# Graph attention on one core: index work in even steps only, edge rows turned between the last node operations

## The chip, the core and the metric

The kernel runs on one core of a Trainium2 chip. Five engines work side by side, each through its own list of instructions in order: TensorE (PE in the profile; PEld are its weight loads), VectorE (DVE), ScalarE (ACT), GpSimd (POOL) and SyncE (SP), which here only issues transfers. The metric is the device time of one execution in microseconds.

## What is computed

6250 nodes with 256 features and 200,000 edges, sorted by destination. The input goes through a layer norm and a Relu to h; then come two layers of graph attention over the edges, with four heads of 64 and with one of 256, and residuals:

```python
def _gat(x, src, dst, ea, Wg, a_s, a_d, Wge, a_e, b, n, h, f):
    hx = (x @ Wg).reshape(n, h, f)
    he = (ea @ Wge).reshape(-1, h, f)
    al = leaky_relu(einsum(hx, a_s)[src] + einsum(hx, a_d)[dst] + einsum(he, a_e), 0.2)
    m = segment_max(al, dst)
    al = exp(al - m[dst])
    al = al / segment_sum(al, dst)[dst]
    out = segment_sum(hx[src] * al[:, :, None], dst)
    return out.reshape(n, h * f) + b
...
te = relu(edge_attr @ We0 + be0) * exp(x @ Wo0 + bo0)[src][:, None]
s2, d2, ea2 = _add_self_loops(src, dst, te, n)
x = relu(_gat(x, s2, d2, ea2, Wg0, ...) + x)
...
x = _gat(x, s2, d2, ea2, Wg1, ...) + x
return x + orig
```

A node's own edge (the self loop) carries the mean of its edges' features.

## The kernel before

A prologue computes the table T of node rows for layer 0 (the 256 transformed features and a few attention terms) and keeps it in HBM. Then each layer goes over the edges in 66 steps: 64 steps of 24 chunks with 128 edges each, and two shorter ones. Every chunk column holds one edge per partition. The method edges (L792) writes out the work of a step k (st) together with preparations for step k + 1 (nx) and what is left of step k - 1 (pv) and k - 2 (late); since the schedule is manual, every engine's list is in the order of that code.

What a step does, in the order of the code, with the engine:

- gather (L1065): 24 indirect transfers, issued on POOL at L1084, bring the source rows of a step's edges from T into one of three buffers G. Since POOL's list runs ahead, it fills the buffer for step k + 2 as soon as the sums of step k - 1 have released it.
- logits (L1367, VectorE): the attention logits al of 24 x 128 edges from G, from rt and from ade, then two scans along the edges (L1390 and L1392) for running maxima per destination.
- ends (L1396, TensorE): turns the last values of each partition into lf.
- spread and parts (VectorE): for a pair of steps at once, in the step before an even one, spread (L1198) builds the one-hots lb (L1210) and Q (L1211) by which destination terms reach the edges; parts (L1315) cuts the destination terms into three bf16 parts (L1325 to L1328). So they stand in odd steps only. TensorE's first product into zad (L1333) waits for them.
- rphase1, rphase2 and adst (TensorE and ScalarE): edge features of step k + 1 through the edge weights, into zad.
- links and maxima (L1401 and L1418, VectorE and TensorE): scans over partitions (L1409, L1411) that read lf, then the maximum per destination; exp on ScalarE.
- scale (L1474, VectorE, L1481) multiplies G by the weights; carried adds what the step before left open; onehots (L1312) builds S, the one-hots of the destinations.
- sums (L1485, TensorE, L1493): 24 products of S and G, each in two passes (48 rows in the trace), summed in PSUM as u; evict copies u on ScalarE.
- the node stage for the step before: finish, which is nodes0 in layer 0 (L1547; merge, then VectorE with one Relu on ScalarE); rows1 to rows3 turn the finished rows and multiply them into the table of layer 1. node_x (L1655) writes x + h into the same row tile t1rows, which goes to HBM.
- edge_rows (L1350, VectorE): turns zad of step k + 1 to rt (L1361) and sums three parts to ade (L1364).

Besides, VectorE prepares index data for the whole of both layers in layer 0: index_group (L738) turns destinations and next destinations of four steps (a group) into the tables loc, flpen, pen and isl, in 14 small operations, most of them 128 x 96. They lie in a generator; index_on (L871), called at the end of a step, issues seven of them. The group is loaded (index_load) when the next group is two steps off or less (left <= 2), which is in every fourth step, k = 0, 4, 8. So seven operations stand at the end of that step, between the node stage and edge_rows, and the rest at the end of the next, odd, step. The logits that follow on VectorE belong to steps k + 1 and k + 2.

Of the kernel before, what the change touches and what calls it, by code (L numbers as in the profile page):

```python
# [81 lines left out]
class Kernel:  # L82
# [425 lines left out]
    def first_edges(self, st, f):  # L508

        if f == 11:  # L510
            st["y"] = self.rphase1(st)
            next(st["y"])
        if f == 12:
            self.spread(st)
            self.parts(st)
        if f == 14:
            self.blocks(st)
            drain(st["y"])
            self.load_ea(1)
        if f == 16:  # L520
            self.rphase2(st)
            self.adst(st)
        if f == 18:
            self.edge_rows(st)
# [213 lines left out]
    def index_group(self, g, pool, di):  # L738
# [8 lines left out]
        t = pool.tile([P, 4 * C], F32, name="gt", bufs=2)  # L747

        def v3(x):
            return x.rearrange("p (s c) -> p s c", c=c)  # L750
# [4 lines left out]
        d3, t3 = v3(dst), v3(t[:, :w])  # L755
        base = self.base_f[:, ss[0]:ss[0] + n].unsqueeze(2).to_broadcast([P, n, c])
        V.tensor_sub(t3, d3, base)
        yield
        V.tensor_scalar(self.loc[:, o:o + w], t[:, :w], 255.0, None, op0=OP.min)
        yield  # L760
        ends = self.before[:, ss[0]:ss[0] + n].unsqueeze(2), v3(dnx)[:, :, c - 1:]
        for pen, e in zip((self.fpen, self.lpen), ends):
            t = pool.tile([P, 4 * C], F32, name="gt", bufs=2)
            e3 = e.to_broadcast([P, n, c])
            V.tensor_sub(v3(t[:, :w]), *((d3, e3) if pen is self.fpen else (e3, d3)))
            yield
            V.tensor_scalar(pen[:, o:o + w], t[:, :w], 1.0, -BIG, op0=OP.min, op1=OP.mult)
            yield
        t = pool.tile([P, 4 * C], F32, name="gt", bufs=2)
        t3 = v3(t[:, :w])  # L770
        V.memset(t3[:, :, 0:1], 1.0)
        V.tensor_sub(t3[:, :, 1:], d3[:, :, 1:], d3[:, :, :c - 1])
        yield
        V.tensor_scalar(self.pen[:, o:o + w], t[:, :w], 1.0, -BIG, op0=OP.min, op1=OP.mult)
        yield
        t = pool.tile([P, 4 * C], F32, name="gt", bufs=2)
        V.tensor_sub(t[:, :w], dnx, dst)
        yield
        V.tensor_scalar(self.isl[:, o:o + w], t[:, :w], 1.0, None, op0=OP.min)
        yield  # L780
        V.tensor_scalar(t[:, :w], t[:, :w], 0.0, None, op0=OP.is_lt)
        yield
        V.tensor_reduce(self.bad[:, 1 + g:2 + g], t[:, :w], axis=AX.X, op=OP.add)
# [8 lines left out]
    def edges(self, ctx):  # L792
# [6 lines left out]
        for k, st in enumerate(steps):  # L799
# [54 lines left out]
            if pv:  # L854
                drain(self.finish(pv))
# [4 lines left out]
            self.index_on(left)  # L860
# [5 lines left out]
            self.edge_rows(nx)  # L866
# [19 lines left out]
    def ending(self, a, b, c, pv, late, after):  # L886
# [43 lines left out]
        self.edge_rows(b)  # L930
# [27 lines left out]
        self.edge_rows(c)  # L958
# [68 lines left out]
        if after:  # L1027
# [22 lines left out]
            self.edge_rows(after)  # L1050
# [299 lines left out]
    def edge_rows(self, st):  # L1350
# [6 lines left out]
        if c % 2:  # L1357
            for w, o in self.halves(st):
                V.transpose(rv[:, w], z[:, o])
        else:  # L1360
            V.transpose(rv[:, :32 * c].rearrange("p (b n) -> p b n", b=2),  # L1361
                        z.rearrange("p (b n) -> p b n", b=2)[:, :, :16 * c])
        st["ade"] = ade = self.wp.tile([P, C, 4], F32, name="ade")
        V.tensor_reduce(ade[:, :c, :H], rt[:, :c, 4:4 + 3 * H].rearrange("p c (h t) -> p c h t", t=3),  # L1364
                        axis=AX.X, op=OP.add)

# [180 lines left out]
    def nodes0(self, st, wp, e=None):  # L1547
# [23 lines left out]
        e.tensor_add(b, a, b)  # L1571
# [4 lines left out]
        yield  # L1576
        st["trow"] = self.trow1[st["s"] % 3]
        if "lag" not in st:
            yield from self.node_x(st, e)
# [18 lines left out]
    def nodes1(self, st, wp, e=None):  # L1598
# [6 lines left out]
        yield  # L1605
# [171 lines left out]
def drain(g):  # L1777
    for _ in g:
        pass
# [85 lines left out]
```

## Time and profile before

| what | value |
|---|---|
| median of 3 runs | 4735.77 us (4732.58 to 4746.24) |
| profiled execution | 4693.76 us, of which the span of the trace 4692.0 |
| mean granted TensorE clock | 0.744 |
| HBM traffic | 591.77 MB, 126 GB/s over the span |
| VectorE instructions | 6211, 2864.4 us busy |
| scale (L1481) | 149 operations, 854.1 us |
| sums (L1493) | 6212 rows, 1719.5 us |
| gathers (L1084) | 3066 issues of 953 ns |

A row of the timeline reads: start in us, duration in us, engine, line, operation, out<-in, shapes, count, and in brackets how long the engine was idle before it and what ended that by the trace; "issue" is a wait for nothing that the trace shows. A row of the view by stretches has, behind the bounds and the length, busy us (and number) of PE, PEld, DVE, ACT and POOL, the granted TensorE clock, the DMA engines' share and GB/s. A row of the view of waits has the total, the number of waits and the longest. Ends of TensorE's rows are modelled, their starts are measured. Line numbers are those of the kernel before.

### The profile page before, as it was taken

Reading aid. Unit: us, or ns where it says so; the run is one execution under the profiler, and the core shown is the slowest. Engines: PE = TensorE matmul, PEld = TensorE weight load, DVE = VectorE, ACT = ScalarE, POOL = GpSimd, SP = SyncE. Lnnn points to the kernel's source line nnn. Section 1 sums busy time; section 2 is a strip of 40 time slices with the busy share of each in tenths; the row PEclk is TensorE's granted clock in tenths of the full one; section 3 lists DMA queues with packets and bytes.
Section 4 is the critical chain, followed back from the end, with each engine's and each line's share of the span. In section 5 each row is a group of like instructions: output and inputs, shape, how many; then the busy total and the mean of one; then the engine's idle time right before and its main releaser. Section 6 shows DMA issues by size and latency. Waiting matters only on the chain.

```text
span 4692.0 us, 35121 instructions
## 1 busy us (share of the span) xinstructions
PE 2924.1 (62%) x10096; PEld 1849.2 (39%) x10096; DVE 2864.4 (61%) x6211; ACT 531.9 (11%) x1189; POOL 2996.0 (64%) x3216
## 2 busy tenths in 40 slices
PE   7666666666666666666666665665556566565666
PEld 5433343343334334344344343333334334333333
DVE  6666676666666666676675554545555455554546
ACT  4211111111111111111110000000000000000000
POOL 5466666666666666666646666666666666666664
PEclk8877777777777777777788676667777766776667
DMA  7344444444444444444444444444444444444442
GB/s 223 89 133 130 127 131 136 123 136 137 124 134 135 125 134 138 125 133 134 122 123 123 118 120 121 124 120 118 126 115 123 122 124 119 118 125 114 122 127 74
DMA packets 248234, 591.77 MB, mean 126 GB/s; under 512 B 65849, under 2 KB 105125, under 8 KB 247783
## 3 DMA queue, kind: packets, MB, share of 16 engines
q0 software_dynamic: 150048, 422.51, 34.5%
q1 hardware_dynamic: 97009, 164.82, 10.9%
q10 hardware_dynamic: 976, 2.12, 0.2%
q8 instruction: 81, 1.33, 0.1%
q14 instruction: 120, 0.98, 0.1%
HBM read 544.23 MB, written 45.36 MB: 126 GB/s over the span
## 4 chain that ended last, share of the span: by engine, by line
DVE 41%; PE 22%; issue 17%; another core or an unknown queue 15%; POOL 2%; ACT 1%; DMA 1%; DVEq 0%; ACTq 0%
DVE G L1481 14%; PE u L1493 14%; DVE S L1312 5%; PE y L1186 3%; POOL G L1084 2%; DVE rt L1361 2%; DVE lb L1210 1%; DVE m L1431 1%; PE ps L570 1%; PE zad L1195 1%; DVE cl L1409 1%; DVE cl L1411 1%; PE fin L570 1%; DVE t1rows L1659 1%
## 5 line engine op out<-in xcount | busy, mean ns | idle before, releaser
L1084 POOL DMA_INDIRECT G<-T,src x3066 | 2920.4, 953 | 1589.9 <-issue 886.1
L1493 PE MATMUL u<-G,S 128*128 128x270 f32 (+1 forms) x6212 | 1719.5, 436 | 700.3 <-issue 501.6
L1493 PEld LDWEIGHTS u<-G,S 128*128 128x128 f32 x6212 | 1324.7, 216 | 1042.7 <-issue 532.5
L1481 DVE TENSOR_TENSOR G<-G,kps 128x6144 f32<-128x6144 f32 (+6 forms) x149 | 854.1, 5739 | 0.0
L1186 PE MATMUL y<-ea,webd 64*128 64x256 f32 (+2 forms) x1056 | 452.1, 799 | 402.8 <-issue 395.1
L1409 DVE TENSOR_TENSOR_SCAN cl<-fl,cl,lf 4x129 f32<-4x129 f32 (+1 forms) x130 | 61.1, 470 | 901.1 <-remote 547.7
L1312 DVE TENSOR_TENSOR S<-kps,loc 128x3072 f32<-128x3072 f32 (+1 forms) x135 | 438.0, 3245 | 4.6
L1195 PE MATMUL zad<-R,wea 128*64 128x384 f32 (+1 forms) x1056 | 294.3, 697 | 154.8 <-ACT R L1187 97.2
L1186 PEld LDWEIGHTS y<-ea,webd 64*128 64x128 f32 x1056 | 159.7, 281 | 531.5 <-issue 519.6
L1499 ACT ACTIVATE U<-u 128x270 f32<-128x270 f32 (+1 forms) x130 | 51.2, 394 | 2037.2 <-remote 1168.4
L1187 ACT ACTIVATE R<-y,webd 128x1024 f32<-128x1024 f32 (+3 forms) x264 | 235.4, 892 | 368.2 <-PE y L1186 169.4
L1195 PEld LDWEIGHTS zad<-R,wea 128*64 128x64 f32 x1056 | 85.0, 181 | 411.9 <-ACT R L1187 205.9
L1361 DVE STREAM_TRANSPOSE rt<-zad 128x768 f32<-128x768 f32 (+1 forms) x130 | 125.8, 968 | 0.8 <-PE zad L1347 0.8
L570 PE MATMUL fin<-wg,h1T 128*128 128x260 f32 x264 | 124.2, 619 | 3.1 <-ACT h1T L1586 3.1
L1333 PE MATMUL zad<-a,Q 128*128 128x12 bf16 (+1 forms) x132 | 24.0, 182 | 156.0 <-issue 81.4
L1399 PE MATMUL lf<-ident,fb 128*36 128x128 f32 (+1 forms) x132 | 44.1, 334 | 112.4 <-DVE fb L1392 51.1
L1210 DVE TENSOR_TENSOR lb<-lb,kps 128x1536 bf16<-128x1536 bf16 (+1 forms) x68 | 112.9, 1660 | 0.0
L1584 PE MATMUL fin<-ident,fb 128*128 128x128 f32 x132 | 43.2, 385 | 82.3 <-issue 81.2
L1524 ACT ACTIVATE mw<-mw,mg 128x2 f32<-128x2 f32 x66 | 19.7, 298 | 607.7 <-DVE mw L1520 390.8
L1416 PE MATMUL lf<-ident,cl 36*128 36x36 f32 (+1 forms) x132 | 38.7, 293 | 76.6 <-DVE cl L1411 76.2
L1347 PE MATMUL zad<-lb,aq 128*128 128x384 bf16 (+2 forms) x264 | 86.0, 419 | 0.0
L1416 PEld LDWEIGHTS lf<-ident,cl 36*128 36x128 f32 (+1 forms) x132 | 22.9, 173 | 158.2 <-DVE cl L1411 155.4
(264 smaller groups left out, 2273.4 us busy)
## 6 DMA issues: line engine op xcount, KB each, us to landing
ea<-in_ea_dram SPq DMA_DIRECT2D x64, 768.0 KB
G<-T,src POOLq DMA_INDIRECT x3066
lb<-locrow SPq DMA_DIRECT2D x64, 384.0 KB
nd<-t1rows SPq DMA_DIRECT2D x66, 225.8 KB
tw<-nd SPq DMA_DIRECT2D x66, 225.8 KB
tw<-T SPq DMA_DIRECT2D x66, 117.2 KB
T<-t1rows SPq DMA_DIRECT2D x66, 113.8 KB
tw<-in_x_dram SPq DMA_DIRECT2D x66, 112.0 KB
```

The lines of the kernel that those rows point to most:

```text
L570: self.product = self.nc.tensor.matmul(ps[:, :L.MW], hT[:, k, :], self.wg[L.l][:, k, :], start=(k == 0), stop=(k == 1))
L1084: g = nc.gpsimd.indirect_dma_start(out=G[:, c, 0:L.TW], out_offset=None, in_=st.get("from", self.T[L.l])[0:self.N, :], in_offset=bass.Indi ...
L1186: nc.tensor.matmul(y[:, i, :n], self.webd[l][r, :], ea[r, w], start=True, stop=True)
L1187: nc.scalar.activation(R[:, :, w], y[:, :, :n], AF.Relu, bias=self.be[l])
L1195: nc.tensor.matmul(st["zad"][i * PH:(i + 1) * PH, o], self.wea[l][0], R[:, i, w], start=True, stop=False)
L1210: V.tensor_tensor(lb[:, :, :n], lb[:, :, :n], self.k_part.unsqueeze(2).to_broadcast([P, i, n]), op=OP.is_equal)
L1312: nc.vector.tensor_tensor(st["S"][:, c0:c1, :], self.k_iota.unsqueeze(1).to_broadcast(w), self.loc[:, o + c0:o + c1].unsqueeze(2).to_broad ...
L1347: self.nc.tensor.matmul(st["zad"][:, o], st["aq"].rearrange("p k j -> p (k j)"), st["lb"][:, w], start=False, stop=True)
L1361: V.transpose(rv[:, :32 * c].rearrange("p (b n) -> p b n", b=2), z.rearrange("p (b n) -> p b n", b=2)[:, :, :16 * c])
L1409: V.tensor_tensor_scan(cl[:H, :], fl[:H, :], lf[:H, 0:P + 1], init, op0=OP.add, op1=OP.max)
L1481: nc.vector.tensor_tensor(v, v, pw[:, c0:c1, :].unsqueeze(3) .to_broadcast([P, c1 - c0, H, L.F]), op=OP.mult)
L1493: p = nc.tensor.matmul(st["u"][:, :L.W], S[:, i, :], G[:, i, 0:L.W], start=(j == 0), stop=(j == c - 1))
```

## The change

1. Index work is issued elsewhere. index_on is called twice in a step: once behind logits and ends, where it acts only in even steps, and once where it stood, where it acts only in the first two steps and when a group must be finished. The load is issued a step earlier (left <= 3).
2. The 14 operations are ordered anew, so that hardly any stands right behind one that it needs: three subtractions first, then three that use them, and so on. The third temporary is the memory of the loaded indices.
3. edge_rows is a generator with a stop behind the transposes and one behind the reduction. finish says where a gap may be filled (yield True), and edges puts the two pieces into the gaps of the node stage; in the other places edge_rows is drained at once.
4. In nodes0 the Relu reads the sum in a (fa) and writes b (fb). The row for layer 1 is made by one operation that clamps a itself and adds x + h, in place of an addition that reads the Relu's result.

```diff
-            if self.rest is None and left <= 2:
+            self.fresh = self.rest is None and left <= 3
+            if self.fresh:
                 gi = self.index_load(self.ahead, self.xp)
...
                 drain(self.logits(st))
                 self.ends(st)
+                self.index_on(k, left, False)
             self.spread(nx)
...
-            if pv:
-                drain(self.finish(pv))
+            rows = self.edge_rows(nx)
+            for gap in self.finish(pv) if pv else ():
+                if gap:
+                    next(rows, None)
+            drain(rows)
             self.evict(st)
...
-            self.index_on(left)
+            self.index_on(k, left, True)
...
-            self.edge_rows(nx)
...
-    def index_on(self, left):
-        if self.rest is not None:
-            for _ in range(7):
-                next(self.rest, None)
-            if left <= 0:
-                drain(self.rest)
-                self.ahead, self.rest = self.ahead + 1, None
+    def index_on(self, k, left, late):
+        if self.rest is None or (left > 0 and k > 1 if late else k % 2 or k < 2 or self.fresh):
+            return
+        for _ in range(7):
+            next(self.rest, None)
+        if left <= 0:
+            drain(self.rest)
+            self.ahead, self.rest = self.ahead + 1, None
...
         e.tensor_add(a, a, hw)
         yield
-        e.tensor_add(b, a, b)
-        if e is V:
-            self.nc.scalar.activation(b, b, AF.Relu)
-        else:
-            e.tensor_scalar(b, b, 0.0, None, op0=OP.max)
-        yield
         st["trow"] = self.trow1[st["s"] % 3]
+        nrow = st["trow"][:, self.L[1].TW:self.L[1].TW + D]
         if "lag" not in st:
-            yield from self.node_x(st, e)
+            e.tensor_add(nrow, xw, hw)
+        yield True
+        e.tensor_add(a, a, b)
+        self.nc.scalar.activation(b, a, AF.Relu)
+        yield True
+        if "lag" not in st:
+            e.scalar_tensor_tensor(nrow, a, 0.0, nrow, op0=OP.max, op1=OP.add)
```

Two places of VectorE's list show it. The first is the end of the node stage in the first step of a group; before, from the last sum of the node stage (fb) over the index operations (gf, gt, loc, flpen) to the edge rows (rt, ade):

```order
L1571 TENSOR_TENSOR fb<-fa,fb 128x256
L1659 TENSOR_TENSOR t1rows<-tw_203,hw 128x256
L1661 TENSOR_TENSOR t1rows<-t1rows,fb 128x256
L752 CAST gf<-gi 128x192
L757 TENSOR_TENSOR gt<-gf,base 128x96
L759 TENSOR_SCALAR loc<-gt 128x96
L765 TENSOR_TENSOR gt<-gf,before 128x96
L767 TENSOR_SCALAR flpen<-gt 128x96
L765 TENSOR_TENSOR gt<-gf 128x96
L767 TENSOR_SCALAR flpen<-gt 128x96
L1361 STREAM_TRANSPOSE rt<-zad 128x768
L1364 TENSOR_REDUCE ade<-rt 128x96
```

The same place after the change; the numbers of the lines are those of the changed kernel, in which logits begin at L1377:

```order
L1571 TENSOR_TENSOR fa<-fa,hw 128x256
L1576 TENSOR_TENSOR t1rows<-tw_203,hw 128x256
L1361 STREAM_TRANSPOSE rt<-zad 128x768
L1578 TENSOR_TENSOR fa<-fa,fb 128x256
L1365 TENSOR_REDUCE ade<-rt 128x96
L1582 SCALAR_TENSOR_TENSOR t1rows<-fa,t1rows 128x256
L1377 TENSOR_TENSOR G<-rt,G 128x24x4
L1379 TENSOR_TENSOR al<-G 128x24x4
```

The seven index operations are gone from here, and transposes and reduction each have a node operation behind them. The second place is that between the logits of an even step and its links (cl); before, for a step that is the first of a group:

```order
L1377 TENSOR_TENSOR al<-G 128x24x4
L1379 TENSOR_TENSOR al<-al,ade 128x24x4
L1381 SCALAR_TENSOR_TENSOR al<-al 128x96
L1390 SCALAR_TENSOR_TENSOR fb_195<-pen_183,al 128x96
L1392 SCALAR_TENSOR_TENSOR fb_195<-pen_183,al 128x96
L1409 SCALAR_TENSOR_TENSOR cl_189<-fl,cl_190,lf 4x129
```

And after the change, again in a step that is the first of a group:

```order
L1394 SCALAR_TENSOR_TENSOR fb_195<-pen_183,al 128x96
L751 CAST gf<-gi 128x192
L760 TENSOR_TENSOR gt_6389<-gf,base 128x96
L760 TENSOR_TENSOR gt_6390<-gf,before 128x96
L760 TENSOR_TENSOR gi<-gf 128x96
L762 TENSOR_SCALAR loc<-gt_6389 128x96
L765 TENSOR_SCALAR flpen<-gt_6390 128x96
L765 TENSOR_SCALAR flpen<-gi 128x96
L1411 SCALAR_TENSOR_TENSOR cl_189<-fl,cl_190,lf 4x129
```

Seven operations now stand in front of links; the other seven stand at the same place two steps later. The lists of TensorE and POOL keep their order. On SP the two loads of the indices stand a step earlier.

More of the change, by code (lines that the diff above doesn't have):

```diff
@@ L754, in index_group @@
         dst, dnx = df[:, 0, :w], df[:, 1, :w]
-        d3, t3 = v3(dst), v3(t[:, :w])
+        d3 = v3(dst)
         base = self.base_f[:, ss[0]:ss[0] + n].unsqueeze(2).to_broadcast([P, n, c])
-        V.tensor_sub(t3, d3, base)
-        yield
-        V.tensor_scalar(self.loc[:, o:o + w], t[:, :w], 255.0, None, op0=OP.min)
-        yield
[L761 to L765, printed above, removed]
-            yield
-            V.tensor_scalar(pen[:, o:o + w], t[:, :w], 1.0, -BIG, op0=OP.min, op1=OP.mult)
-            yield
@@ L769, in index_group @@
[L769 to L772, printed above, removed]
+        first = self.before[:, ss[0]:ss[0] + n].unsqueeze(2).to_broadcast([P, n, c])
+        end = v3(dnx)[:, :, c - 1:].to_broadcast([P, n, c])
+        t = [pool.tile([P, 4 * C], F32, name=f"gt{i}", bufs=1)[:, :w] for i in range(2)] + [di[:, 0, :w].bitcast(F32)]
+        for x, y, z in zip(t, (d3, d3, end), (base, first, d3)):
+            V.tensor_sub(v3(x), y, z)
+            yield
@@ L1049, in ending @@
                 next(fill, None)
-            self.edge_rows(after)
+            drain(self.edge_rows(after))
             drain(fill)
```

30 lines of the change are left out of this document (17 added, 13 removed).

## The prediction

> **What bounds the kernel now.** The page comes first: the busy share of each engine and the chain that ended last.
>
> ```profile
> PE 2924.1 (62%) x10096; PEld 1849.2 (39%) x10096; DVE 2864.4 (61%) x6211; ACT 531.9 (11%) x1189; POOL 2996.0 (64%) x3216
> DVE 41%; PE 22%; issue 17%; another core or an unknown queue 15%; POOL 2%; ACT 1%; DMA 1%; DVEq 0%; ACTq 0%
> ```
>
> No engine is full, and a third of the chain is waiting. So the question is how long a step takes and what ends it. The view by stretches, one stretch of layer 0 and one of layer 1:
>
> ```profile
> 437.41:2339.74 1902.33, 1198.07 (x4052) 755.67 (x4051) 1269.88 (x2788) 230.47 (x541) 1232.80 (x1297) 0.76 0.47 131
> 2588.04:4577.04 1989.00, 1204.61 (x4006) 743.41 (x4006) 1069.63 (x2031) 152.56 (x291) 1327.54 (x1392) 0.70 0.45 121
> ```
>
> POOL issues 24 gathers a step, so these are 1297 / 24 = 54 steps of layer 0 at 35.23 us and 1392 / 24 = 58 steps of layer 1 at 34.29 us. VectorE is busy 23.5 us of a step in layer 0 and 18.4 us in layer 1: 5 us more work costs only 0.94 us. The excess is not spread evenly, as POOL's first gather of five successive steps shows in the timeline (the last column is POOL's wait before it):
>
> ```profile
> 1001.36 0.94 POOL L1084 DMA_INDIRECT G<-T,src  x1 [4.73 <-PE fin L1584]
> 1035.69 0.94 POOL L1084 DMA_INDIRECT G<-T,src  x1 [4.65 <-PE fin L1584]
> 1073.18 0.94 POOL L1084 DMA_INDIRECT G<-T,src  x1 [7.85 <-PE fin L1584]
> 1107.50 0.94 POOL L1084 DMA_INDIRECT G<-T,src  x1 [4.35 <-PE fin L1584]
> 1142.30 0.94 POOL L1084 DMA_INDIRECT G<-T,src  x1 [5.05 <-PE u L1493]
> ```
>
> The steps last 34.33, 37.49, 34.32 and 34.80 us. POOL fills the third gather buffer and must wait until the sums on TensorE (u<-G,S) have released it, so its restart marks the end of a step's sums. I call that moment the restart. What happens before it, in an ordinary step, on TensorE:
>
> ```profile
> 1084.78 13.44 PE L1493 MATMUL u<-G,S 128*128 128x270 f32 x46 [4.56 <-DVE crow L1469]
> 1100.62 0.61 PE L1493 MATMUL u<-G,S 128*128 128x270 f32 x1 [2.40 <-issue]
> 1103.43 0.61 PE L1493 MATMUL u<-G,S 128*128 128x270 f32 x1 [2.20 <-issue]
> ```
>
> The sums start 11.6 us after the restart at 1073.18. 46 of the 48 run at 0.29 us each, until 25 us after the restart; then one takes 2.8 us, though it waits for nothing that is shown. This slow stretch ends shortly before the next restart, and layer 1 has it too, there with the next step's first products in it:
>
> ```profile
> 3506.94 0.58 PE L1186 MATMUL y<-ea,webd 64*128 64x256 f32 x1 [2.64 <-issue]
> 3513.00 0.95 POOL L1084 DMA_INDIRECT G<-T,src  x1 [4.54 <-remote]
> ```
>
> VectorE is slow in it as well, wherever an operation waits for its own predecessor. Sums that start in time end inside the stretch and cost nothing more; sums that start late have a remainder behind it. That is the long step:
>
> ```profile
> 1050.94 8.70 PE L1493 MATMUL u<-G,S 128*128 128x270 f32 x37 [1.51 <-DVE crow L1469]
> 1068.67 4.23 PE L1493 MATMUL u<-G,S 128*128 128x270 f32 x8 [1.49 <-issue]
> ```
>
> Its sums start 15.25 us after the restart, eight are left at 1068.67, and the next restart comes 3.2 us late. Why they start late is told by VectorE around that restart:
>
> ```profile
> 1025.31 0.26 DVE L757 TENSOR_TENSOR gt<-gf,base 128x96 f32<-128x96 f32 x1 [2.83 <-issue]
> 1026.71 0.21 DVE L759 TENSOR_SCALAR loc<-gt 128x96 bf16<-128x96 f32 x1 [1.14 <-issue]
> 1028.81 0.27 DVE L767 TENSOR_SCALAR flpen<-gt 128x96 bf16<-128x96 f32 x1 [1.73 <-remote]
> 1031.62 0.21 DVE L767 TENSOR_SCALAR flpen<-gt 128x96 bf16<-128x96 f32 x1 [2.38 <-issue]
> 1031.75 0.98 DVE L1361 STREAM_TRANSPOSE rt<-zad 128x768 f32<-128x768 f32 x1
> 1036.41 0.33 DVE L1392 TENSOR_TENSOR_SCAN fb<-pen,al 128x96 f32<-128x96 bf16 x1
> 1036.66 1.73 DVE L1210 TENSOR_TENSOR lb<-lb,kps 128x1536 bf16<-128x1536 bf16 x1
> 1039.34 0.47 DVE L1409 TENSOR_TENSOR_SCAN cl<-fl,cl,lf 4x129 f32<-4x129 f32 x1
> ```
>
> Seven index operations of a quarter of a microsecond stand in the slow stretch, four of them behind one that they need, and those wait 8.08 us together. Edge rows and logits come after them, the logits end 0.7 us behind the restart, and then the spread of an odd step stands before links: links' first scan (cl) starts 3.65 us after the restart. Two and three steps on it starts 0.15 and 0.40 us after the restart:
>
> ```profile
> 1107.65 0.47 DVE L1409 TENSOR_TENSOR_SCAN cl<-fl,cl,lf 4x129 f32<-4x129 f32 x1
> 1137.28 0.34 DVE L1392 TENSOR_TENSOR_SCAN fb<-pen,al 128x96 f32<-128x96 bf16 x1
> 1142.70 0.47 DVE L1409 TENSOR_TENSOR_SCAN cl<-fl,cl,lf 4x129 f32<-4x129 f32 x1 [5.09 <-PE zad L1333]
> ```
>
> The first of these rows is the odd step without index work before it, with the same spread; in the even step at 1142 VectorE stands idle for 5.09 us between logits and links.
>
> **The change part by part.** *Index work moved.* Of each group of four steps, the second (odd) one no longer has seven index operations ahead of its edge rows. Its logits and its spread can then end as in the odd step at 1107, so that links start at the restart and the sums 11.6 us after it, as at 1084.78. POOL's waits at the first and the last of the 14 long steps of this kind between 437 and 2340 us are:
>
> ```profile
> 509.51 0.94 POOL L1084 DMA_INDIRECT G<-T,src  x1 [7.98 <-PE u L1493]
> 2339.74 0.94 POOL L1084 DMA_INDIRECT G<-T,src  x1 [6.46 <-PE u L1493]
> ```
>
> An ordinary wait is that of layer 1, in the view of who waited for whom in the same stretch as above:
>
> ```profile
> POOL G L1084 <- remote: 149.7, 34, 4.6
> POOL G L1084 <- PE y L1186: 95.2, 22, 4.8
> ```
>
> 244.9 us over 56 waits are 4.37 us. The three long steps quoted stand 3.61, 3.48 and 2.09 us above it, 3.06 on average: 14 x 3.06 = 43 us less. The bounds: all of the excess of layer 0 is 54 x 0.94 = 51 us in this stretch, so the long steps can't give more than that; taking only the cheapest of the three, 14 x 2.09 = 29 us.
>
> *Index work added behind the even steps' logits.* There, VectorE is free for 5.09 us, TensorE being busy with sums, transposes and lf. Seven operations at one per 1.4 us (the spacing of the rows at 1025.31 and 1026.71) would need 9.8 us if all lay in the slow stretch; 5.09 / 1.4 = 3.6, so about four fit before it ends, and three are left for 3 x 0.27 = 0.8 us beside TensorE's own last pieces. What waits behind them on VectorE is the links scan, and behind that TensorE's transposes, the scale and the sums. Cost: 0 to 0.8 us in each of the 27 even steps of the 54, 0 to 22 us; I take 0.1 us, 3 us in all, since the next part makes the cover longer. Without that cover the seven cost 7 x 0.27 = 1.9 us.
>
> *Edge rows between the last node operations.* Before, in the order of VectorE:
>
> ```profile
> 1126.26 0.44 DVE L1571 TENSOR_TENSOR fb<-fa,fb 128x256 f32<-128x256 f32 x1
> 1127.97 0.43 DVE L1661 TENSOR_TENSOR t1rows<-t1rows,fb 128x256 f32<-128x256 f32 x1 [0.94 <-DVE t1rows L1659]
> 1128.31 0.98 DVE L1361 STREAM_TRANSPOSE rt<-zad 128x768 f32<-128x768 f32 x1
> 1130.70 0.45 DVE L1364 TENSOR_REDUCE ade<-rt 128x96 f32<-128x288 f32 x1 [1.41 <-DVE rt L1361]
> 1133.51 0.32 DVE L1377 TENSOR_TENSOR al<-G 128x96 f32<-128x96 f32 x1 [2.18 <-issue]
> ```
>
> The count stays the same. The wait for the Relu on ScalarE (0.94 us in front of L1661; the view names the operation before it) goes, since the last node operation clamps by itself, and the reduction no longer stands behind its transposes (1.41 us): logits start up to 2.4 us earlier. On the path this counts only where logits and spread are late without index work. One such step:
>
> ```profile
> 824.79 0.94 POOL L1084 DMA_INDIRECT G<-T,src  x1 [4.40 <-PE fin L1584]
> 826.78 0.47 DVE L1409 TENSOR_TENSOR_SCAN cl<-fl,cl,lf 4x129 f32<-4x129 f32 x1
> 860.49 0.95 POOL L1084 DMA_INDIRECT G<-T,src  x1 [5.78 <-PE u L1493]
> ```
>
> Links start 1.99 us after the restart, and POOL's next wait is 1.41 us above the ordinary one. The excess that the long steps leave is 51 - 43 = 8 us; I take 6 us of it. The Trainium skill speaks against this part (VectorE: DVE Perf Modes, "The DRAIN you can't avoid" and "Rules for kernel authors"): a chain with a semaphore after each operation is said to take as long as one without, so only the number of operations counts, not their distance. By that rule this term would be 0 and the sum 6 us smaller; the waits of 1.41 and 2.18 us in the slow stretch of this trace differ from it.
>
> *The rest.* Relu reads a and runs later on ScalarE, in front of the eviction, which waits for the sums anyway: 0. The index loads are issued a step earlier, and SP's queue has no wait behind them that others wait for: 0. TensorE's and POOL's orders don't change. In layer 1, VectorE has 16 us free a step: 0.
>
> The sum: 43 - 3 + 6 = 46 us. The profiled execution took 4693.76 us (span 4692.0) and would take 4648. The median of the runs shown is 4735.77, 42 us more, and no view shows where these lie; I take the same 46 us off it: 4690 us, 1.0% faster.
>
> **The rivals.** *Slower: the index work comes too late in the even steps.* If it were issued only after the slow stretch ends, together with what logits still owe, links would start as late in 27 even steps as now in the long ones, +3.06 us each: 27 x 3.06 - 46 = 37 us more, 4773 us. For it speaks that the logits of the other even step of a group have no such gap in front of links; they end 0.14 us behind the restart at 1073.18:
>
> ```profile
> 1072.99 0.33 DVE L1392 TENSOR_TENSOR_SCAN fb<-pen,al 128x96 f32<-128x96 bf16 x1
> ```
>
> Against it: they are late because index work stood before their edge rows in the long step, and just that goes. It decides from 46 / 27 = 1.7 us of delay per even step.
>
> *No change: POOL sets the pace.* POOL is the busiest engine at 64%; 34.33 us of an ordinary step less its wait of 4.65 are 29.7 us of gathers, which the change leaves alone, and if they set the step the time stays at 4736 us. The Trainium skill says as much (Perfetto Trace Analysis, "Identifying the Most-Contended Engine": the engine with the highest occupancy is the one to optimise first). Against it: POOL's own wait grows from 4.65 to 7.85 us just where links is late, so there POOL is held by TensorE. A delay of 1.7 us in the even steps gives this time too.
>
> *The spread alone makes odd steps long.* Then moving index work would give only the 6 us of the third part and lose 3: 4733 us. The odd step at 1107 with its spread and 34.80 us speaks against it.
>
> **The numbers.** About 0.3% (14 us) is what a measurement can tell. Forecast, a gain of more than 14 us: 0.87; POOL or the spread: 0.09; slower: 0.04. The range: the cheapest long steps less the dearest even steps leave 29 - 22 = 7 us, 4729; I stop at the border of no change, 4722, which leaves 1.3 in 10 above; the lower end is all excess of layer 0 (57 steps, with three alike before the stretch: 54 us), and 14 us more, as far as the runs of this kernel lie apart: 4735.77 - 54 - 14 = 4668.
>
> **What would show it.** Right: POOL restarts in layer 0 every 34.2 to 34.8 us, with no step of 37; links' first scan within 0.7 us of the restart in every step; logits ended 3 us or more before it; index operations between them and links, in even steps alone; layer 1 unchanged at 34.29. Wrong: even steps of 36 us with VectorE busy at the restart, or odd steps still long with the spread as what links follows.

## The result, and the profile after

The changed kernel takes 4694.35 us (median of 4 runs, 4690.43 to 4703.82), the kernel before beside it 4734.88 us (4732.58 to 4746.24): ratio 0.9913, 95% interval 0.99 to 0.9925, 40.5 us less. The forecast was 4690 us. The profiled execution of the changed kernel took 4691.18 us (span 4689.3), in line with its other runs. That of the kernel before had taken 4693.76 us, 41 us under its median. So the two traces are only 2.7 us apart, and where the time went must be read from the steps, not from the spans.

The page of the changed kernel, busy time and chain:

```profile
PE 2936.1 (63%) x10096; PEld 1851.6 (39%) x10096; DVE 2834.2 (60%) x6211; ACT 534.1 (11%) x1189; POOL 3000.1 (64%) x3216
DVE 31%; PE 24%; issue 19%; another core or an unknown queue 14%; POOL 10%; ACT 1%; DMA 1%; SPq 0%; DVEq 0%; ACTq 0%; POOLq 0%
```

VectorE's share of the chain fell from 41% to 31%, and POOL's rose from 2% to 10%. The view by stretches, between the restarts that answer to those of before:

```profile
439.45:2323.49 1884.04, 1188.67 (x4050) 748.92 (x4048) 1257.19 (x2778) 230.30 (x541) 1235.44 (x1296) 0.76 0.48 133
2574.56:4573.76 1999.20, 1215.24 (x4006) 747.55 (x4006) 1054.42 (x2031) 154.95 (x291) 1328.86 (x1392) 0.71 0.44 120
```

54 steps of layer 0 take 34.89 us each (35.23 before): 18.3 us less in this trace. 58 steps of layer 1 take 34.47 us (34.29 before), 10.2 us more. There too the edge rows now stand between the last two node operations, but VectorE stands idle in front of links for 15.86 us (before, at 3512.80), so its order should not count. The median even step of layer 0 rose by as much, from 34.32 to 34.49 us. So 0.18 us a step is taken below for a difference between the two executions; no run shows that it is one. POOL's restarts in the timeline of the changed kernel, at the place that was quoted of before and at one that did worse:

```profile
683.37 0.94 POOL L1084 DMA_INDIRECT G<-T,src  x1 [4.82 <-PE u L1495]
719.89 0.94 POOL L1084 DMA_INDIRECT G<-T,src  x1 [6.83 <-PE u L1495]
...
1035.33 0.94 POOL L1084 DMA_INDIRECT G<-T,src  x1 [5.72 <-PE u L1495]
1069.99 0.94 POOL L1084 DMA_INDIRECT G<-T,src  x1 [4.97 <-PE fin L1587]
1104.42 0.94 POOL L1084 DMA_INDIRECT G<-T,src  x1 [4.52 <-PE fin L1587]
1139.68 0.94 POOL L1084 DMA_INDIRECT G<-T,src  x1 [5.20 <-PE u L1495]
```

The step at 1035, a long one of 37.49 us before, lasts 34.66 us; the odd step at 1104 without index work, 34.80 us before, lasts 35.26 us, and the one of that kind at 683 lasts 36.52. Taken together by their place in a group of four, from all 54 steps of each trace:

| place in a group of four | steps | before, mean us | after, mean us | all of them, us |
|---|---|---|---|---|
| even, ahead of the long step | 14 | 34.35 | 34.67 | +4.6 |
| odd, the long step before | 14 | 37.20 | 34.79 | -33.8 |
| even, behind the long step | 13 | 34.33 | 34.65 | +4.2 |
| odd, with the spread but no index work before | 13 | 34.95 | 35.47 | +6.8 |

Behind the means lie two kinds of steps: 39 of the 54 last 34.37 to 34.95 us after the change, 15 last 35.17 to 36.57. Seven of the 15, all of the last kind in the table, have sums that start late, 11.9 us or more after the restart. In the other eight, five of them even, the sums start on time, 11.2 to 11.5 us after the restart; but only 40 to 44 of the 48 run at the full rate, and two or three are left at the end. Such sums, in the even step of 35.67 us that starts at 1835.42:

```profile
1846.59 9.38 PE L1495 MATMUL u<-G,S 128*128 128x270 f32 x40 [1.23 <-issue]
...
1869.31 1.51 PE L1495 MATMUL u<-G,S 128*128 128x270 f32 x3 [1.49 <-issue]
```

VectorE behind the logits of an even step and at the end of the next (odd) one, in the timeline of the changed kernel:

```profile
1065.98 0.33 DVE L1394 TENSOR_TENSOR_SCAN fb<-pen,al 128x96 f32<-128x96 bf16 x1
1066.24 0.24 DVE L768 TENSOR_TENSOR gt<-gf 128x92 f32<-128x92 f32 x1
1069.43 0.21 DVE L772 TENSOR_SCALAR pen<-gt 128x96 bf16<-128x96 f32 x1 [2.78 <-remote]
1069.80 0.25 DVE L778 TENSOR_REDUCE bad<-gi 128x1 f32<-128x96 f32 x1
1070.14 0.47 DVE L1411 TENSOR_TENSOR_SCAN cl<-fl,cl,lf 4x129 f32<-4x129 f32 x1
...
1091.93 0.45 DVE L1365 TENSOR_REDUCE ade<-rt 128x96 f32<-128x288 f32 x1 [1.66 <-remote]
1093.33 0.42 DVE L1582 SCALAR_TENSOR_TENSOR t1rows<-fa,t1rows 128x256 f32<-128x256 f32 x1 [0.95 <-issue]
1093.70 0.26 DVE L1377 TENSOR_TENSOR G<-rt,G 128x96 f32<-128x96 f32 x1
1098.23 0.32 DVE L1379 TENSOR_TENSOR al<-G 128x96 f32<-128x96 f32 x1 [4.27 <-remote]
1102.03 0.33 DVE L1394 TENSOR_TENSOR_SCAN fb<-pen,al 128x96 f32<-128x96 bf16 x1
1104.96 0.47 DVE L1411 TENSOR_TENSOR_SCAN cl<-fl,cl,lf 4x129 f32<-4x129 f32 x1
```

The index work does lie between the even step's logits and links, takes one wait of 2.78 us there and is done 0.1 us before links' first scan, which starts 0.15 us after the restart. The odd step's edge rows now stand between node operations, but the reduction still waits 1.66 us, and the logits' second operation waits 4.27 us. VectorE's waits over the stretch 437.41 to 2339.74 us, of the kernel before:

```profile
DVE ade L1364 <- DVE rt L1361: 42.1, 36, 1.4
DVE t1rows L1661 <- remote: 39.0, 19, 2.1
DVE al L1377 <- remote: 37.2, 17, 2.9
DVE t1rows L1661 <- DVE t1rows L1659: 35.2, 30, 1.6
...
DVE al L1377 <- issue: 17.4, 8, 2.2
```

and of the changed one:

```profile
DVE al L1379 <- remote: 172.7, 41, 4.3
DVE al L1379 <- issue: 47.2, 12, 4.3
...
DVE ade L1365 <- remote: 28.2, 17, 1.7
DVE t1rows L1582 <- issue: 21.8, 23, 1.0
DVE t1rows L1582 <- DVE ade L1365: 20.9, 26, 1.0
DVE ade L1365 <- DVE fa L1578: 20.6, 23, 1.5
```

The wait of one logits operation (L1377 before, L1379 after) grew from 55 us in 25 steps to 220 us in 53, 4.1 us a step. What the earlier start of the logits won is given back there: from the node stage's first large operation (fa) to the start of the logits' last scan, the 26 steps of the table's last two rows took 13.4 us on average before the change and 13.9 after it.

### The profile page after: what moved, and what is told of

Same layout as the page of the kernel before. It is cut to its first block, busy times and chain, and to the rows that moved or that the text cites. A ratio compares the mean times of both kernels' runs of the same rounds, so it can differ in the third digit from the quotient of the medians.

```text
span 4689.3 us, 35036 instructions
## 1 busy us (share of the span) xinstructions
PE 2936.1 (63%) x10096; PEld 1851.6 (39%) x10096; DVE 2834.2 (60%) x6211; ACT 534.1 (11%) x1189; POOL 3000.1 (64%) x3216
## 4 chain that ended last, share of the span: by engine, by line
DVE 31%; PE 24%; issue 19%; another core or an unknown queue 14%; POOL 10%; ACT 1%; DMA 1%; SPq 0%; DVEq 0%; ACTq 0%; POOLq 0%
PE u L1495 16%; DVE G L1483 12%; POOL G L1084 10%; DVE S L1312 4%; PE y L1186 3%; DVE lb L1210 1%; DVE m L1433 1%; DVE rt L1361 1%; PE ps L570 1%; PE fin L570 1%; PE zad L1195 1%; DMA G<-T,src 1%; DVE al L1379 1%; DVE a3r L1326 1%
## 5 line engine op out<-in xcount | busy, mean ns | idle before, releaser
L1379 DVE TENSOR_TENSOR al<-G 128x96 f32<-128x96 f32 (+1 forms) x132 | 34.2, 259 | 236.6 <-remote 176.3
L1587 PEld LDWEIGHTS fin<-ident,fb 128*128 128x128 f32 x132 | 24.7, 195 | 164.7 <-issue 160.1
```

The costliest lines, as they stand in the source:

```text
L1379: V.tensor_add(zv, gr, G[:, :c, L.p:L.p + H])
```

## The experiments

In all of them the kernel before, timed beside each, takes 4027 us, not 4735. They ran on three chips (numbers 5, 11 and 13), which agree; on which chip the runs at 4735 us fell isn't known. What the difference is due to isn't known; it made the experiments another test than planned. Each part of the change was first tried alone on the kernel before, then in a form of it in which POOL has less to do.

**The kernel before, again.**

> The kernel before, unchanged, as the measure for the other three. Ratio 1.000 within 0.002. Open point: the profiled execution of before took 4693.76 us where its timed runs took 4732 to 4746. If the long steps are the whole cause of the change's gain, this trace should show 14 steps of layer 0 whose links start 3.6 us or more after POOL's restart, steps of 37 us there, and 34.3 to 34.5 us in layer 1. If the 42 us lie in the long steps, these are 3 us longer here than in the first trace; if they lie everywhere, layer 1 is 0.3 us a step longer.

4027.26 us against 4026.89 (ratio 1.0001, 0.9992 to 1.001). Its view by stretches, chain and VectorE's two largest waits from 437.41 to 1900 us:

```profile
437.41:1900.00 1462.59, 997.80 (x3635) 654.25 (x3634) 1145.74 (x2496) 204.17 (x485) 1107.92 (x1165) 0.83 0.56 153
```

```profile
POOL 45%; DVE 24%; issue 17%; PE 7%; DMA 6%; ACT 1%; DVEq 0%; POOLq 0%; SPq 0%; ACTq 0%
```

```profile
DVE G L1375 <- DMA G<-T,src: 224.9, 48, 8.9
DVE mg L1538 <- ACT mw L1536: 13.4, 49, 0.3
```

1462.59 / 1165 x 24 = 30.1 us a step, in which POOL's gathers follow each other with 0.3 us between them and POOL waits for nothing longer; VectorE waits for the last gather's data 4.7 us a step, and the view lists no wait for its own operations. The slow stretch isn't there, and so the 42 us that the expectation asks about can't be looked for. All this speaks for POOL setting the pace; the thinned kernel below tests it.

**The new order of the index operations alone, at their old place.**

```diff
-        V.tensor_sub(t3, d3, base)
-        yield
-        V.tensor_scalar(self.loc[:, o:o + w], t[:, :w], 255.0, None, op0=OP.min)
-        yield
...
+        for x, y, z in zip(t, (d3, d3, end), (base, first, d3)):
+            V.tensor_sub(v3(x), y, z)
+            yield
+        V.tensor_scalar(self.loc[:, o:o + w], t[0], 255.0, None, op0=OP.min)
```

> Of the change, only the new order of the 14 index operations; they stay where they were, seven in front of the edge rows. Theory (the place counts: seven operations in the slow stretch delay logits, whatever their order): the first index operations still take 6 us or more of the slow stretch, links in the long steps still start 2 us or more after the restart; gain 0 to 15 us, ratio 0.997 to 1.000. Rival (the distance counts: each wait of an operation for the one just before it costs 1.1 to 2.8 us): the four waits of 8.08 us shrink to about two, logits end 4 us earlier, the long steps vanish; gain 40 us, ratio 0.9915. Second rival (the Trainium skill, VectorE: DVE Perf Modes, Rules for kernel authors: only the count of operations matters): no difference at all, 1.000.

4025.44 us, ratio 0.9997 (0.9988 to 1.0006). This decides between none of the three: where POOL sets the pace, no order of VectorE's operations can show.

**The new place alone, twice.**

```diff
                 drain(self.logits(st))
                 self.ends(st)
+                self.index_on(k, left, False)
...
-            self.index_on(left)
+            self.index_on(k, left, True)
```

> Of the change, only the place: index operations in their old order behind the logits of even steps; edge rows and node stage as before. Theory: the long steps vanish, gain 40 us, ratio 0.9915; even steps wait up to 0.8 us more, since in the old order four of the seven stand right behind one that they need. Rival (edge rows and the Relu carry the gain): less than 15 us. Rival (even steps take the delay over): links in even steps start 1.7 us or more after the restart, ratio 1.000 or above.

4030.51 us, ratio 1.0008 (0.9999 to 1.0017).

> Only the place of the index work changed, once more, because the four runs before it fell on a chip on which the same kernel takes 4027 us, has no slow stretch and lets POOL gather without a break (30 us a step). If this chip has the slow stretch (the kernel before at 4730 us): theory, the long steps vanish, ratio 0.9915, 40 us; rival (edge rows and Relu carry the gain), 0.997 or more. If it has none: POOL sets the pace and the ratio lies between 0.999 and 1.002, as measured there.

4030.35 us, ratio 1.0007 (0.9998 to 1.0017). The case without a slow stretch came out as expected (0.999 to 1.002); what the place is worth in a slow stretch stays undecided.

**Edge rows and the Relu alone.**

```diff
-                drain(self.finish(pv))
+            rows = self.edge_rows(nx)
+            for gap in self.finish(pv) if pv else ():
+                if gap:
+                    next(rows, None)
+            drain(rows)
...
+        e.tensor_add(a, a, b)
+        self.nc.scalar.activation(b, a, AF.Relu)
...
```

> Of the change, only the edge rows between the last node operations and the Relu off the path; index work in its old place and order, now behind the edge rows and in front of logits. Theory: transposes and reduction leave the slow stretch, the seven index operations stay; logits in the long steps end 2 to 3 us earlier, links start 1 to 2 us after the restart in place of 3.65; gain 20 to 30 us, ratio 0.9937 to 0.9958. Rival (the index operations alone are what delays): links still at 3.6 us, gain under 10 us. Rival (edge rows carry it all): gain 40 us.

4027.66 us, ratio 1.0001 (0.9992 to 1.001): none of the three cases, which all speak of the slow stretch, could be tested here.

**The whole change there.**

> The changed kernel once more, beside the kernel before, on the chip that this run gets. Theory (the place of the index work counts only where the gathers' restart waits for TensorE's sums, as in the trace of before at 35.2 us a step): where the kernel before takes about 4735 us, the ratio is 0.991 again; where it takes about 4027 us and POOL issues its gathers back to back (30.0 us a step in the control), the ratio is 1.000 within 0.001 and both orders cost the same. Rival (the gain is of another kind, such as fewer VectorE waits that count everywhere): 0.990 to 0.993 there too, some 30 to 40 us.

4027.44 us, ratio 1.0002 (0.9993 to 1.0011). VectorE's largest wait in the same stretch as above:

```profile
DVE G L1377 <- DMA G<-T,src: 273.6, 48, 9.3
```

The first theory holds: no part moves the time, and neither does the whole. VectorE is finished 49 us earlier in 48 steps and waits 49 us longer for the gathers (273.6 - 224.9). The rival "POOL sets the pace" was right about this place, and it says nothing about the one where 40 us were won.

**POOL taken off the path.** To make VectorE and TensorE set the step here, 8 of the 24 gathers of 58 steps of layer 0 were replaced by one contiguous load (the texts below say 48 steps; the trace has 58 such loads, and 2602 gathers in place of 3066). Those columns hold other rows of the table, so other values come out; the work of VectorE and TensorE and the bytes stay.

```diff
+            nc.sync.dma_start(G[:, 0:n, 0:L.TW],
+                              self.T[0][0:n * P, :].rearrange("(p j) w -> p j w", j=n)[:, :, 0:L.TW])
+            cols = (last, *range(n, last))
```

> The kernel before, with 8 of the gathers of each of 48 steps of layer 0 replaced by one contiguous load of as many rows through SyncE's queue (those columns then hold other rows of the table, so what is computed from them differs; the amount of work on VectorE, TensorE and of bytes is the same). POOL's work in a step falls by 8 x 1.25 = 10 us. If POOL sets the pace on this chip, a layer-0 step falls from 30.0 us until the next bound, VectorE (23.5 us busy in a step there), so to 24 to 27 us: the kernel is 140 to 290 us faster than before, and POOL's gathers wait again for a buffer that TensorE's sums free. If VectorE or the transfers set it, it gains under 50 us.

> The changed kernel with the same 8 gathers replaced by a load in 48 steps. To be compared with the kernel before under the same thinning, run beside it. Theory: with POOL off the path, the long steps (7 index operations in front of the edge rows) set the restart late again and the new place saves 1 to 3 us in each of 14 steps, so 14 to 42 us less than the thinned kernel before. Rival (VectorE's busy time alone sets a step then, wherever the operations stand): the two within 8 us. Rival (the new order loses where VectorE is full, since the index work delays the links in 27 even steps): 8 us or more slower.

The thinned kernel before: 3775.82 us (3774.78 to 3777.49), ratio to the unthinned one 0.9379 (0.9366 to 0.9392). The thinned changed kernel: 3736.37 us (3734.9 to 3737.62), ratio 0.9281 (0.9268 to 0.9294). Both numbers lie where the theories put them. POOL was the bound, and between 400 and 1690 us it now waits for TensorE before 50 steps, 5.8 us each:

```profile
POOL G L1090 <- PE fin L1590: 287.7, 50, 7.5
```

With POOL out of the way the change is worth 39.5 us; that the new place is what saves them, as the second theory says, is not what its parts show further down. Four steps of each, from scale to scale, in the view by stretches; first the thinned kernel before:

```profile
1013.74:1039.25 25.51, 19.50 (x75) 13.44 (x75) 24.09 (x53) 4.22 (x11) 14.89 (x16) 0.87 0.69 213
1039.25:1063.57 24.32, 18.18 (x75) 12.63 (x75) 21.56 (x47) 4.22 (x11) 15.46 (x16) 0.93 0.58 151
1063.57:1090.79 27.22, 18.68 (x73) 13.17 (x75) 25.66 (x59) 4.12 (x10) 17.55 (x19) 0.90 0.71 217
1090.79:1115.46 24.67, 19.87 (x79) 12.66 (x77) 22.81 (x53) 4.31 (x11) 13.17 (x15) 0.91 0.59 139
```

then the thinned changed kernel:

```profile
994.89:1019.84 24.95, 18.34 (x75) 12.64 (x75) 23.74 (x52) 4.22 (x11) 15.66 (x17) 0.93 0.71 214
1019.84:1045.36 25.52, 19.38 (x75) 13.47 (x75) 22.39 (x54) 4.21 (x11) 14.87 (x16) 0.87 0.62 161
1045.36:1070.42 25.06, 18.74 (x75) 12.88 (x75) 23.72 (x52) 4.33 (x11) 15.39 (x17) 0.86 0.67 202
1070.42:1094.55 24.13, 18.00 (x75) 12.54 (x75) 22.22 (x53) 4.10 (x11) 14.92 (x16) 0.93 0.63 151
```

The long step is here too: 27.22 us, with 59 VectorE operations (spread and seven index operations), and it is gone after the change. The even step that had no index work before (47 operations, 21.56 us of VectorE work) carries seven index operations afterwards and does not pay for all of them, since links wait there for TensorE. Such a scan in the thinned kernel before, and in the changed one with the index work ahead of it:

```profile
1060.08 0.47 DVE L1415 TENSOR_TENSOR_SCAN cl<-fl,cl,lf 4x129 f32<-4x129 f32 x1 [1.42 <-PE zad L1339]
```

```profile
1041.87 0.47 DVE L1417 TENSOR_TENSOR_SCAN cl<-fl,cl,lf 4x129 f32<-4x129 f32 x1 [1.97 <-PE zad L1339]
```

**The parts, thinned.** The edits are those shown above, on the thinned kernel before.

> The thinned kernel before (8 gathers of 48 steps replaced by one load, so other rows in those columns), with one part of the change alone: edge rows between the last operations of the node stage and the Relu on ScalarE; the index work as in the kernel before. The traces of the two thinned kernels show VectorE without a gap; from the node stage's first large operation to the logits they show 3.79 us in an ordinary step (1027.48 to 1031.27) and 3.24 us with the change (1008.60 to 1011.84), 0.55 us less. Theory (each operation that no longer follows the one it needs is worth its 0.1 to 0.2 us in every step where VectorE sets the pace): 52 x 0.55 = 28 us of the 39 us, so 3747 us, and the index work gives the other 11. Rival (the place of the index work is the gain, as the prediction had it, 43 of 46 us): 3 to 8 us, so 3768 to 3773 us.

3762.9 us (3760.31 to 3765.67), ratio 0.9344 (0.9332 to 0.9357): 12.9 us less than the thinned kernel before, between theory (28) and rival (3 to 8), so neither holds. What the 0.55 us a step of the expectation is made of is seen in the rows of the node stage and the logits, of the thinned kernel before and of the thinned changed kernel:

```profile
1027.48 0.42 DVE L1573 TENSOR_TENSOR fa<-tw,mw 128x256 f32<-128x256 f32 x1
1031.27 0.26 DVE L1381 TENSOR_TENSOR G<-rt,G 128x96 f32<-128x96 f32 x1
```

```profile
1008.60 0.42 DVE L1575 TENSOR_TENSOR fa<-tw,mw 128x256 f32<-128x256 f32 x1
1011.84 0.25 DVE L1383 TENSOR_TENSOR G<-rt,G 128x96 f32<-128x96 f32 x1
```

With no slow stretch about, the eight operations from the one row to the other take 3.24 us in place of 3.79. Of the difference, 0.22 us is the wait for the Relu: in the thinned kernel before, ScalarE's Relu ends at 1029.49, and the last node operation starts at 1029.52, 0.56 us behind the one before it, where 0.34 us is usual. The other 0.33 us goes where an operation no longer stands right behind one that it needs. The Trainium skill (VectorE: DVE Perf Modes, "The DRAIN you can't avoid") says that in a chain of eight copies a semaphore after each costs nothing extra. These rows don't fit the reading that only the number of operations counts: the number is the same.

> The thinned kernel before with the place of the index work alone (only in even steps behind the logits, from three steps ahead; the old order of its operations and the old edge rows). Theory (edge rows give most, above): the 1.35 us that 7 index operations take in front of the edge rows leave VectorE's row and lie in its wait of 1.4 to 2 us for TensorE ahead of the links' scan, but only in even steps, where that wait is, so 14 groups x 0.5 to 1.3 us, 7 to 18 us less than the thinned kernel before, so 3758 to 3769 us. Rival (the place gives nearly all): 35 to 43 us less, 3733 to 3741 us. Rival (the even steps pay for it): 3776 us or more.

3776.87 us (3772.61 to 3777.08), ratio 0.9376 (0.9363 to 0.9389): no difference from the thinned kernel before, against the 7 to 18 us that the theory wanted and the 35 to 43 of the first rival; the second rival, that the even steps pay for it (3776 us or more), holds. Two of its steps, which the others repeat:

```profile
1009.61:1035.53 25.92, 18.35 (x75) 12.61 (x75) 24.27 (x53) 4.33 (x11) 16.54 (x18) 0.93 0.70 210
1035.53:1060.81 25.28, 19.15 (x75) 13.30 (x75) 22.92 (x53) 4.01 (x11) 14.00 (x15) 0.86 0.62 154
```

The long steps are gone, and yet four steps take 102.4 us, as before (102.4 by the means of its steps). The even steps grew by 0.56 us on average, and their 48 sums now take 13.8 us, where the thinned kernel before took 13.3 in even steps without index work and 12.9 in those with it. The odd steps that were not long grew by 0.25.

> The thinned kernel before with the new order of the index operations alone, at their old place. Seven of them took 1.35 us in the old order (1004.84 to 1006.19) and 1.2 us in the new one (1038.68 to 1039.88). Theory: 28 such stretches x 0.15 = 4 us less than the thinned kernel before, 3772 us; at most 10. Rival (the waits of an operation for the one before it are what cost): 15 us or more.

3778.37 us (3776.14 to 3779.36), ratio 0.9379 (0.9366 to 0.9392): nothing, not the 4 us expected.

> The thinned changed kernel (8 gathers of 48 steps replaced by one load, so other rows in those columns) with the index operations in their old order: edge rows between the node stage's operations and the index work behind the logits in even steps, together. Alone these two gave 13 us and -1 us of 39, and in the traces of both a longer step is followed by one whose links' scan waits for TensorE (up to 3.2 us with the edge rows alone). Theory (in a pair of steps one is set by VectorE's row and the other by TensorE's sums, and only both parts together shorten both): 33 to 39 us less than the thinned kernel before, 3737 to 3743 us, and the order gives the few us that are left. Rival (the order of the index operations is needed for it): over 3750 us. Rival (the parts add up, and something else made the difference): about 3764 us.

3736.28 us (3734.67 to 3741.48), ratio 0.9279 (0.9266 to 0.9292): the whole 39.5 us, without the new order. The first theory holds. Edge rows alone give 12.9 us, the place alone nothing, and both together three times their sum. Where this comes from is told by the 49 or 50 steps that start between 395 and 1640 us in each trace, mean us from scale to scale:

| step | thinned before | edge rows alone | place alone | both |
|---|---|---|---|---|
| even, no index work in it | 24.70 | 24.86 | none | none |
| even, with index work | 24.70 | 24.48 | 25.26 | 24.72 |
| odd, no index work in it | 25.67 | 25.10 | 25.92 | 25.11 |
| odd, with index work (long) | 27.29 | 26.99 | none | none |
| all | 25.59 | 25.33 | 25.60 | 24.92 |

Over 58 steps the last row makes 15 us less with the edge rows, nothing with the place and 39 us less with both, close to the measured 12.9, none and 39.5. Two odd steps with the edge rows alone, without index work and with it:

```profile
1006.46:1031.40 24.94, 18.34 (x75) 12.55 (x75) 23.73 (x52) 4.21 (x11) 15.66 (x17) 0.93 0.71 213
...
1056.99:1083.95 26.96, 18.92 (x75) 13.12 (x75) 25.43 (x60) 4.13 (x10) 16.95 (x18) 0.85 0.67 201
```

With the edge rows alone, the odd steps without index work come down, but the long ones by 0.3 us only. With the place alone, the long ones come down, but only to the 25.92 us that an odd step takes with the old edge rows, and the other steps give that back. Only with both do all odd steps take 25.1 us on average. The even steps' links wait for TensorE's sums in each of these kernels, with the edge rows alone for up to 3.2 us:

```profile
1053.50 0.47 DVE L1419 TENSOR_TENSOR_SCAN cl<-fl,cl,lf 4x129 f32<-4x129 f32 x1 [3.16 <-PE zad L1341]
```

What VectorE wins ahead of links in an even step goes into that wait: in even steps without index work it is 1.8 us on average in the thinned kernel before and 2.5 with the edge rows alone. Index work put there is covered by it in part. Why the sums of the even steps are slower with the place alone, and not with both, these runs don't show; so that the two parts help each other is shown, and why is shown only in part.

## Why the prediction was right, and where it wasn't

- **What binds.** Late index work, late logits, late links, late sums, late restart: the chain is confirmed by the trace. With the index work out of them, the 14 long steps went from 37.20 to 34.79 us, and links' first scan starts at most 0.7 us after the restart in 50 of the 54 steps (29 of 54 before). No step of 37 us is left. One reading was off: the logits were said to end 0.7 us behind the restart at 1035.69, but that is the start of their last scan, which ends 1.05 us behind it. And one rule did not hold: that sums which start in time cost nothing more. In eight of the 15 steps over 35 us they start on time and still end late, and why isn't shown.
- **Index work moved, 43 us (29 to 51).** The long steps gave 33.8 us in the traces, or 36.3 if 0.18 us a step, by which layer 1 ran slower in this execution, is added to them (14 x 0.18 = 2.5). Inside the bounds, but the mean of 3.06 us from three long steps was too high: over all 14 it is 37.20 - 34.79 = 2.4.
- **Even steps, 3 us lost (0 to 22).** They lost 8.8 us by the traces, or 4 after taking off the same 0.18 a step. But the index work delayed nothing: links start at most 0.41 us after the restart in all 27 even steps. What is left of the loss lies in five even steps of 35.17 to 35.67 us, whose sums started on time, so the size came out near without its reason. The slower rival is out: its price was 3.06 us for each of 27 steps, and the even steps got 0.32 longer.
- **Edge rows, 6 us won: this step failed.** The prediction put the gain in the odd steps without index work. They got slower, by 0.52 us each, 6.8 us in all (4.5 after taking off the 0.18). The waits that were to go did not go. The last node operation (t1rows), which no longer needs the Relu, still waits 44 us in 50 steps, where it had waited 79 us in 52; the reduction, with a node operation in front of it, waits 57 us in 45 steps, where it had waited 51 in 41 (all rows of each in the view of waits). And the logits met a wait of 4.1 us a step in the slow stretch. Their end was to lie 3 us or more before the restart, and does so in 28 of 54 steps; in an odd step the spread comes on top. The rival "the spread alone makes odd steps long" came true in a small way: seven steps of this kind last 35.26 to 36.57 us, with sums that start 11.9 us or more after the restart.
- **The sum.** 46 us were forecast; the runs gave 40.5, the two traces show 18.3 in layer 0, or 28 with the 0.18 added for 54 steps. Some 12 to 22 us of the measured gain are thus not found in the traces. The kernel before was profiled in an execution 41 us faster than its median, the changed kernel in one 3 us faster; this was noticed in the prediction and is still unexplained, so the kernel before may have run its steps otherwise in the timed executions than in the trace. The terms were 43, -3 and 6 us; the traces give 33.8, -8.8 and -6.8. That the median came within 5 us of the forecast is therefore in part luck: the same 46 us were taken off it, and the 42 us between it and the trace were not understood.
- **The rivals.** That POOL sets the pace is wrong where the forecast was made (POOL still waits 4.5 to 6.8 us at the restarts shown) and right where the experiments ran, to within 0.1%. The page of the kernel before in that place has POOL as the busiest engine over the span:

```profile
PE 2743.2 (68%) x10096; PEld 1781.2 (44%) x10096; DVE 2869.4 (71%) x6211; ACT 531.2 (13%) x1189; POOL 2989.8 (74%) x3216
```

  So there the Trainium skill's rule (Perfetto Trace Analysis, "Identifying the Most-Contended Engine") agrees with the run: taking work from POOL alone gave 6.2%. In the stretch of layer 0 shown above it would name VectorE, though, which is busier there (1145.74 us against 1107.92) and was not the bound.
- **What stays open.** No part was run alone where 40.5 us were won: all runs of parts fell where the kernel before takes 4027 us. That the long steps were the gain there, and that the edge rows gave nothing, is read from the traces of before and after. In the thinned runs the edge rows were needed for the gain; whether they are needed at 4735 us too wasn't measured.

## What to carry to other kernels

Look for the operation that stands in front of the critical one in every fourth step only: a step that is 3 us longer than its neighbours shows a wrong place where averages of busy time show nothing. When two engines take turns in setting the step, measure two small edits together before giving up either of them: here 13 us and 0 us made 39.5. And a gain off a path that another engine sets is no gain at all: the same edit was worth 0.9% where POOL waited for TensorE, and 0.0% (ratio 0.9993 to 1.0011) where POOL never waited more than 0.3 us between gathers.

## What the runs showed of the hardware

- The same program took 4735 us in one set of runs and 4027 us in another, with a mean granted clock of 0.744 and 0.796 in the profiled executions. The clock isn't all of it, as it differs by 7% and the time by 18%: in the slower set, an operation of VectorE that needs the one before it waits 1.1 to 2.8 us late in the gathers of a step, in the faster one the view of waits has no such row, though POOL issues a gather in 951 to 953 ns in both.
- In that slow stretch, putting one operation between two that depend on each other didn't remove the wait: the reduction waited 51 us in 41 steps before, right behind its transposes, and 57 us in 45 steps after, with a node operation between.
- The granted clock differs from step to step. In the four steps shown of the thinned changed kernel it was 0.93, 0.87, 0.86 and 0.93, and their 48 sums took 12.9, 14.1, 13.3 and 12.7 us.
